# Spreading vector work over the slots of a hand-written order: the first token half behind the last gate and up chunks

## The chip, the cores and the metric

The kernel runs on one core of a Trainium2 chip. Its engines work side by side, each through its own queue of instructions, in order: TensorE (PE in the profile, with the load of its weights shown apart as PEld), VectorE (DVE), ScalarE (ACT), GpSimd (POOL) and SyncE (SP), which here only issues DMA transfers. They wait for each other through semaphores.

The metric is the device time of one execution in microseconds (us), as the median of several runs. A profile is one execution taken by the hardware profiler. Its span runs from the first to the last instruction.

## The reference

Input `x` has 8 batches of 256 tokens with 1024 features, all in float32. Four layers with low-rank adapters (LoRA, rank 16) follow each other, and each adds its result to `x`. Every batch picks its own adapter in each layer.

```python
# layer 0
x = x + (x @ W.T + b + 2.0 * ((x @ A0[id0]) @ B0[id0]))
# layer 1, hidden width F = 2752
gate = x @ W_gate.T + 0.5 * ((x @ A_gate[id1].T) @ B_gate[id1].T)
up   = x @ W_up.T   + 0.5 * ((x @ A_up[id1].T)   @ B_up[id1].T)
act  = silu(gate) * up
x = x + (act @ W_down.T + 0.5 * ((act @ A_down[id1].T) @ B_down[id1].T))
# layers 2 and 3, adapters alone
x = x + (x @ B2[id2].T) @ A2[id2].T
x = x + (x @ B3[id3].T) @ A3[id3].T
```

## The kernel before

**Tiling.** The 2048 tokens are taken in two blocks of 1024 (`blk` 0 and 1), and each block in two halves of 512 tokens (`n` 0 and 1). Layer 0 is done for both blocks, then for each block gate and up, then the down projection with layers 2 and 3. Gate and up are cut along F into chunks of 128; groups of four chunks make a job (`g` 0 to 4). What is left, 64 columns more than 21 chunks, is the remainder: `rest()`, the "last gate and up chunks", named `r` in tile names (`pa_r`, `c_r_X`). It is computed first, ahead of group 0.

**Products.** The large matrix products use a Strassen-like scheme with seven products in place of eight, on two levels. In gate and up the outer seven products are seven units, in the order 1, 2, 3, 5, 6, 7, 4, and each unit's inner seven products are issued by `step` in the order 1, 5, (4 of the unit before), 6, 3, 2, 7. An inner product of a group is four matmuls of 128 x 256; one of the remainder is two. The profile shows each matmul as two records. Inner products write the PSUM banks `pa` (two banks in turn), `pc` and `pb` (one bank each), and each is then added to a result in SBUF (`c_X`, `c_E`, `c_Z`, `c_Y`) by VectorE (lines 509 and 512) or copied there by ScalarE (line 288). Line 478 is the matmul itself. Product 4 of a unit is put into `pending` and issued by `flush()` in slot 2 of the next unit, which also calls `done` when that unit completes a result.

**The remainder's end.** When gate and up of a half are complete (`both` in `done`), these follow: four 32-row expands, one in each group of 32 rows (`lora`, tile `plr`, line 994), into four banks of the pool `ps_l`, which has four; four sums of them onto gate and up (lines 1175, 1176, and 1179 twice); Sigmoids on ScalarE (`gates`); four multiplies (line 1172), of which the last two write `hr`; and `hidden`, a memset, and for the second half also the down-rank products (`shrink_hidden`, tile `pd`, line 263). Before its `lora`, each half needs `trep`: eight ScalarE copies into two banks of `ps_l` and two VectorE multiplies (`spread`, line 1138). The first half completes after remainder unit 5 of 7 (product 6), the second after the last (product 4).

**The order of work.** Each unit has slots, and `at(slot)` first calls what was hooked to the slot, and then takes items from the queue `beside` until their costs reach the unit's share:

```python
            spent = 0
            while beside and spent < u.share:
                cost, f = beside.popleft()
                f()
                spent += cost
```

A cost is a number of the order alone and not a time. An item `(9, lambda: None)` does nothing and uses up the slot. The share is 0.2 or 0.3 in the last remainder units, and 1.1 and 0.8 in the first two units of group 0. So one item of 0.69 fills a slot of the remainder, and two fill a slot of group 0.

The text gives this order; the instructions on an engine may still be placed otherwise by the framework's scheduler, which keeps dependencies. In the kernel before, VectorE's queue has the first half's sums and its first multiply as lines 1175, 1179, 1172, 1176, 1179, while the text calls 1175, 1176, 1179, 1179, 1172.

**Transfers.** Tokens come from DRAM (`toks`) into tiles `tk`, weights into `w_...`, issued by SyncE, one unit or more ahead, into a pool of 22 large buffers that rotate; a load waits until the buffer's last user is done. GpSimd forms the weight sums `sw` (lines 448 to 451) and `w_B`, `w_T` (line 439), one unit ahead, the sums of the down weights `wo` in block 0 (lines 772 to 775), and gathers the adapters' rows (`bgu`, `ad`; line 233), each into two buffers in turn.

Of the kernel before, what the change touches and what calls it, by code (L numbers as in the profile page):

```python
# [54 lines left out]
def kernel(  # L55
# [48 lines left out]
    nc = tc.nc  # L104
# [14 lines left out]
    def big(name):  # L119
        return upool.tile([P, BIG], F32, tag="u", name=name)  # L120

    def bank(pool, name):
        return pool.tile([P, 512], F32, tag=pool.name, name=name)
# [116 lines left out]
    def gather_a(table, layer, blk, name, pool=apool, tag="a", width=NC * R):  # L240
        t = pool.tile([P, BB * width], F32, tag=tag, name=name)
        t = t[:, : BB * table.shape[1]].rearrange("p (b w) -> p b w", b=BB)
        for q in range(BB):
            b = blk * BB + q
            gather(t[:, q, :], table, off_a[:, layer, b : b + 1])
        return t
# [40 lines left out]
    def copy(dst, src, scale=1.0):  # L287
        nc.scalar.activation(dst, src, AF.Identity, scale=scale)  # L288
# [4 lines left out]
    beside = deque()  # L293
# [666 lines left out]
    def gate_up(blk):  # L960
# [5 lines left out]
        def tables(g):  # L966
            b = bgpool.tile([P, 2, NN, P], F32, tag="bg", name=f"bgu_{blk}_{g}")
            for table in range(2):
                for n in range(NN):
                    gather(b[:, table, n], bgu[g], off_gx[:, blk, table, n : n + 1])  # L970
            st["bgu", g] = b
            chunks = ad[g].shape[1] // R
            st["ad", g] = (
                gather_a(ad[g], 1, blk, f"ad_{blk}_{g}", pool=adpool, tag="ad", width=4 * R),
                chunks,
            )

        def shrink_hidden(g, *halves):

            a, chunks = st["ad", g]  # L980
            pss = []
            for n, h in halves:
                pss.append(bank(ps_l, f"pd_{blk}_{g}_{n}"))
                for r in range(len(h)):
                    shrink_into(pss[-1], r, a, chunks, r, n, h[r], True, True)
            for (n, h), ps in zip(halves, pss):
                rows, td = slice(0, 32 * len(h)), st["td"][n]
                if g == REST:
                    nc.vector.memset(td, 0.0)
                nc.vector.tensor_add(td[rows], td[rows], ps[rows])  # L990

        def expand_gu(table, n, g, r, ps):
            rows = slice(32 * r, 32 * r + 32)
            nc.tensor.matmul(  # L994
                ps,
                st["bgu", g][rows, table, n],
                st["t"][rows, table, n, :],
                start=True,
                stop=True,
                skip_group_check=True,  # L1000
            )
# [102 lines left out]
        def rest():  # L1104

            held = {}

            def raw(key, t):
                kh, table = int(key[1]) - 1, int(key[2]) - 1
                if table == 0:  # L1110
                    nc.sync.dma_start(out=t, in_=wrem[kh, 0])
                    return
                nc.sync.dma_start(out=t[:, :512], in_=wrem[kh, 1, :, :512])

                w = t[:, 512:].rearrange("p (c m) -> p c m", m=P)
                for j in range(2):
                    a = st["agu"][j].rearrange("p b (r c) -> p c (b r)", c=NC)
                    nc.scalar.copy(
                        w[:, :, j * BB * R : (j + 1) * BB * R], a[:, kh * HC : (kh + 1) * HC, :]
                    )  # L1120

            def done(n, table, c):
                c = c.rearrange("p q i j t -> p (q i) (j t)")
                held[n, table] = c
                if "t" not in st:
                    st["t"] = big(f"trep_{blk}").rearrange("p (g n t) -> p g n t", g=2, n=NN)
                    st["hr"] = big(f"hr_{blk}").rearrange("p (c n t) -> p c n t", c=2, n=NN)
                t, hr = st["t"], st["hr"]
                lo = []
                ranks, both = c, (n, 1 - table) in held  # L1130

                def spread(j):

                    src = slice(64 * j + 32 * n, 64 * j + 32 * n + 32)
                    ps = bank(ps_l, f"pt_{blk}_{n}_{j}")
                    for r in range(4):
                        copy(ps[32 * r : 32 * r + 32], ranks[src, 1, :], 0.5)
                    nc.vector.tensor_mul(t[:, j, n, :], ps, mask)

                if table == 1:  # L1140
                    for j in range(2):
                        beside.append((0.69, lambda j=j: spread(j)))
                    if both:

                        for _ in range(6):
                            beside.append((9, lambda: None))
                if not both:
                    return
                g, u = held[n, 0], held[n, 1]

                def lora():

                    for j in range(4):
                        lo.append(bank(ps_l, f"plr_{blk}_{n}_{j}"))
                        expand_gu(j // 2, n, REST, j, lo[j])

                def gates():
                    nc.scalar.activation(lo[0], g[:, 0], AF.Sigmoid)
                    nc.scalar.activation(lo[1][:FR], g[:FR, 1], AF.Sigmoid)

                    copy(u[:FR, 1], g[FR:, 1])

                left = slice(0, FR)

                def hidden():
                    nc.vector.memset(hr[FR:, 1, n], 0.0)
                    held["hr", n] = [hr[:, 0, n], hr[:, 1, n]]
                    if ("hr", 1 - n) in held:
                        shrink_hidden(REST, *((n, held["hr", n]) for n in range(NN)))

                def multiply(to, x, y):
                    beside.append((0.69, lambda: nc.vector.tensor_mul(to(), x(), y())))

                beside.append((0, lora))
                beside.append((0.69, lambda: nc.vector.tensor_add(g[:, 0], g[:, 0], lo[0])))
                beside.append((0.69, lambda: nc.vector.tensor_add(u[:, 0], u[:, 0], lo[2])))
                for j, c in ((3, slice(FR, P)), (1, left)):
                    beside.append(
                        (0.69, lambda j=j, c=c: nc.vector.tensor_add(g[c, 1], g[c, 1], lo[j][c]))
                    )  # L1180
                beside.append((0, gates))
                for a, b, c in ((g[:, 0], 0, slice(0, P)), (g[left, 1], 1, left)):
                    multiply(lambda b=b, c=c: lo[b][c], lambda a=a: a, lambda b=b, c=c: lo[b][c])
                multiply(lambda: hr[:, 0, n], lambda: u[:, 0], lambda: lo[0])
                multiply(lambda: hr[left, 1, n], lambda: u[left, 1], lambda: lo[1][left])
                beside.append((1.2, hidden))

            q = Quads(blk, f"1_{blk}_r", 1, raw, done, SHARE_REST)

            def shrink_tables():  # L1190
                st["agu"] = [
                    gather_a(t, 1, blk, f"agu_{blk}_{j}") for j, t in enumerate((ag, au))
                ]

            q.units[0].ahead.insert(0, (3, 0, shrink_tables))
            q.units[0].before(2, 0, lambda: tables(REST))
# [500 lines left out]
```

## Time and profile before

| | |
|---|---|
| median of 3 runs | 1817.87 us (1817.19 to 1818.16) |
| profiled execution, its own time | 1794.66 us |
| its span | 1792.7 us |
| granted TensorE clock | 0.998 |
| TensorE busy | 1779.4 us (99%) |
| VectorE busy | 1039.3 us (58%) |
| GpSimd busy | 1007.1 us (56%) |
| ScalarE busy | 306.6 us (17%) |
| remainder's end, block 0 and block 1 | about 265 to 288 us and 1044 to 1066 us from the span's start |

A row of the list in order of time shows the start, the duration, the engine, the line, the operation with output and inputs, the count, and in brackets the idle time before it with what ended that. Matmuls are pipelined and their ends are modelled, so a busy TensorE is not one at its peak, and the distance from start to start tells more than a duration. An engine is idle at no cost where TensorE doesn't wait for it.

### The profile page before, as it was taken

The page shows a single profiled execution, that of the slowest core. Times are in us where ns is not written, and L with a number is a line of the kernel's source. Part 1 is how long each engine was busy: PE and PEld are TensorE (multiplying, and loading weights), DVE is VectorE, ACT ScalarE, POOL GpSimd, SP SyncE. Part 2 cuts the span into 40 slices and gives each one's busy share as a digit, 9 for nine tenths or more (in the row PEclk, how much of TensorE's full clock was granted, in tenths as well). Part 3 has the DMA queues.
Part 4 walks back from the last instruction along what each step waited for, and adds up shares of the span by engine and source line. Part 5 has one row for each costly group of instructions (what it writes and reads, how often), then busy time and mean ns, then how long its engine had stood idle before and what let it go on. Part 6 is the DMA issues. An engine that isn't in the chain of part 4 may idle for free.

```text
span 1792.7 us, 20768 instructions
## 1 busy us (share of the span) xinstructions
PE 1779.4 (99%) x7664; PEld 1310.9 (73%) x7664; DVE 1039.3 (58%) x1675; ACT 306.6 (17%) x552; POOL 1007.1 (56%) x807
## 2 busy tenths in 40 slices
PE   9999999999999999999999999999999999999998
PEld 4444477888787888788854678787888887888743
DVE  5584256666666666757842474757575757544623
ACT  0121023020212121224210231111212121221001
POOL 6202579685868677344631777766767564444302
PEclk9999999999999999999999999999999999999999
DMA  6476895867686756678831885575748475645302
GB/s 235 174 282 247 275 393 186 314 223 291 208 298 207 297 182 235 250 270 323 321 128 60 293 325 194 175 281 175 293 169 292 162 259 179 252 168 187 125 0 94
DMA packets 119446, 404.42 MB, mean 226 GB/s; under 512 B 11890, under 2 KB 42738, under 8 KB 109874
## 3 DMA queue, kind: packets, MB, share of 16 engines
q1 hardware_dynamic: 108464, 381.72, 58.7%
q0 software_dynamic: 6288, 13.77, 2.4%
q10 hardware_dynamic: 4594, 7.61, 1.3%
q8 instruction: 62, 1.02, 0.2%
q14 instruction: 38, 0.31, 0.0%
HBM read 318.64 MB, written 84.41 MB: 225 GB/s over the span
## 4 chain that ended last, share of the span: by engine, by line
PE 91%; issue 5%; DVE 3%; POOL 0%; ACT 0%; POOLq 0%; ACTq 0%; DVEq 0%
PE pa L478 27%; PE pc L478 13%; PE pa_d L478 11%; PE pa L377 8%; PE pb L478 6%; PE pc_d L478 5%; PE pc L377 4%; PE pb_d L478 3%; PE pa_r L478 2%; PE pl L994 2%; PE pb L377 2%; PE pp L880 2%; PE pc_r L478 1%; PE pd L263 1%; PE p L263 1%
## 5 line engine op out<-in xcount | busy, mean ns | idle before, releaser
L478 PE MATMUL pa<-tk,sw 128*128 128x256 f32 x1120 | 270.3, 384 | 0.0
L478 PE MATMUL pc<-tk,sw 128*128 128x256 f32 x1120 | 264.6, 379 | 0.0
L478 PEld LDWEIGHTS pa<-tk,sw 128*128 128x128 f32 x1120 | 209.8, 190 | 58.2 <-issue 9.9
L478 PEld LDWEIGHTS pc<-tk,sw 128*128 128x128 f32 x1120 | 212.8, 190 | 28.9
L478 PE MATMUL pa<-tk,w_B 128*128 128x256 f32 x960 | 227.8, 380 | 0.0
L478 PEld LDWEIGHTS pa<-tk,w_B 128*128 128x128 f32 x960 | 181.6, 190 | 32.5 <-issue 8.2
L448 POOL TENSOR_TENSOR sw<-w_B 128x512 f32<-128x512 f32 x60 | 76.4, 1273 | 167.8 <-PE pa L478 148.6
L619 POOL TENSOR_TENSOR dx_d<-dw_d 128x512 f32<-128x512 f32 x28 | 37.3, 1354 | 159.1 <-PE pa L478 41.5
L478 PE MATMUL pb<-tk,w_B 128*128 128x256 f32 x480 | 113.4, 379 | 0.0
L478 PE MATMUL pa_d<-dh_d,dw_d 128*128 128x256 f32 x448 | 102.6, 380 | 0.0
L478 PE MATMUL pc_d<-dh_d,dw_d 128*128 128x256 f32 x448 | 101.6, 379 | 0.0
L478 PEld LDWEIGHTS pb<-tk,w_B 128*128 128x128 f32 x480 | 91.2, 190 | 12.4
L509 DVE TENSOR_TENSOR c_X<-c_X,pa 128x512 f32<-128x512 f32 x90 | 61.3, 681 | 65.2 <-PE pa L478 65.2
L439 POOL TENSOR_TENSOR w_B<-w_B,w_B 128x1024 f32<-128x1024 f32 x40 | 93.5, 2361 | 2.4 <-PE pa L478 2.4
L478 PEld LDWEIGHTS pa_d<-dh_d,dw_d 128*128 128x128 f32 x448 | 85.5, 191 | 12.6 <-issue 0.8
L478 PEld LDWEIGHTS pc_d<-dh_d,dw_d 128*128 128x128 f32 x448 | 85.1, 190 | 11.6
L450 POOL TENSOR_TENSOR sw<-w_B 128x512 f32<-128x512 f32 x60 | 87.7, 1461 | 0.0
L451 POOL TENSOR_TENSOR sw<-w_B,sw 128x512 f32<-128x512 f32 x60 | 80.7, 1345 | 3.9
L449 POOL TENSOR_TENSOR sw<-sw,w_B 128x512 f32<-128x512 f32 x60 | 77.0, 1284 | 0.0
L288 ACT ACTIVATE c_X<-pa 128x512 f32<-128x512 f32 x30 | 17.7, 589 | 340.2 <-PE pa L478 340.2
L233 POOL DMA_INDIRECT ad<-in_ad_dram,off_a x48 | 46.1, 960 | 29.2 <-PE pd L263 18.4
L377 PE MATMUL pa<-ht,wd 128*128 128x512 f32 x128 | 59.6, 598 | 0.0
(386 smaller groups left out, 3133.0 us busy)
## 6 DMA issues: line engine op xcount, KB each, us to landing
tk<-toks SPq DMA_DIRECT2D x140, 896.0 KB, 6.7
w_B<-in_wgu_dram SPq DMA_DIRECT2D x40, 1024.0 KB, 5.1
tk_r<-toks SPq DMA_DIRECT2D x28, 896.0 KB, 9.5
hk<-c_Z SPq DMA_DIRECT2D x32, 512.0 KB, 4.2
dh_d<-hk SPq DMA_DIRECT2D x14, 1024.0 KB, 8.7
hk<-c_Y SPq DMA_DIRECT2D x24, 512.0 KB, 4.6
x1d<-x SPq DMA_DIRECT2D x8, 1024.0 KB, 6.7
wo<-in_wd_dram SPq DMA_DIRECT2D x8, 1024.0 KB, 7.0
```

The source lines that it names most:

```text
L233: nc.gpsimd.indirect_dma_start(out=t, out_offset=None, in_=table, in_offset=bass.IndirectOffsetOnAxis(ap=off, axis=0),)
L263: nc.tensor.matmul(ps[32 * r : 32 * r + 32, :], v, src, start=start, stop=stop, skip_group_check=True)
L377: nc.tensor.matmul(ps, v[j], m[j], start=start and k == 0, stop=k == len(moving) - 1, skip_group_check=True,)
L439: f(self.raw[out][:, c], self.raw[a][:, c], self.raw[b][:, c])
L448: nc.gpsimd.tensor_add(s1, m21, m22)
L449: nc.gpsimd.tensor_sub(s2, s1, m11)
L450: nc.gpsimd.tensor_sub(s3, m11, m21)
L451: nc.gpsimd.tensor_sub(s4, m12, s2)
L478: nc.tensor.matmul(ps[:, q, :], w(j, q, kk), tok(j, kk), start=start and q == 0 and kk == 0, stop=kk == self.deep - 1, skip_group_check=True,)
L509: nc.vector.tensor_add(view(out, r, k), view(old, r, k), ps)
L619: nc.gpsimd.tensor_sub(s3[:, c], a11[:, c], a21[:, c])
L880: nc.tensor.matmul(pss[j, n], st["w", o][:, i, j // HC], x[c][n], start=i == 0, stop=i == NC - 1,)
```

## The change

In `rest()`, each vector operation behind a half's expands is appended through a new helper, `vector`. For the first half (`n == 0`) the helper appends an empty item of cost 9 behind each operation. That makes eight empty items per token block: behind the four sums and the four multiplies. Operands and operations stay as they are, and the second half's items are appended as before.

```diff
+                def vector(f):
+                    beside.append((0.69, f))
+                    if n == 0:
+
+                        beside.append((9, lambda: None))
+
                 def multiply(to, x, y):
-                    beside.append((0.69, lambda: nc.vector.tensor_mul(to(), x(), y())))
+                    vector(lambda: nc.vector.tensor_mul(to(), x(), y()))
 
                 beside.append((0, lora))
-                beside.append((0.69, lambda: nc.vector.tensor_add(g[:, 0], g[:, 0], lo[0])))
-                beside.append((0.69, lambda: nc.vector.tensor_add(u[:, 0], u[:, 0], lo[2])))
+                vector(lambda: nc.vector.tensor_add(g[:, 0], g[:, 0], lo[0]))
+                vector(lambda: nc.vector.tensor_add(u[:, 0], u[:, 0], lo[2]))
                 for j, c in ((3, slice(FR, P)), (1, left)):
-                    beside.append(
-                        (0.69, lambda j=j, c=c: nc.vector.tensor_add(g[c, 1], g[c, 1], lo[j][c]))
-                    )
+                    vector(lambda j=j, c=c: nc.vector.tensor_add(g[c, 1], g[c, 1], lo[j][c]))
                 beside.append((0, gates))
```

## The prediction

> **What bounds the kernel now.** I read the page first, for the bound, then the list of the matmul engine's work in order of time around the place that is edited, then the same stretch for all engines.
>
> ```profile
> span 1792.7 us, 20768 instructions
> ...
> PE 1779.4 (99%) x7664; PEld 1310.9 (73%) x7664; DVE 1039.3 (58%) x1675; ACT 306.6 (17%) x552; POOL 1007.1 (56%) x807
> ...
> PE 91%; issue 5%; DVE 3%; POOL 0%; ACT 0%; POOLq 0%; ACTq 0%; DVEq 0%
> ```
>
> TensorE is busy for 99% of the span and holds 91% of the chain that ended last, at a granted clock of 0.998. So an edit is worth what it adds to or takes from TensorE's own sequence; VectorE (DVE) counts only where TensorE waits for it. Next, TensorE alone, at the end of the last gate and up chunks of token block 0 (start, duration, instruction):
>
> ```profile
> 276.08 1.03 PE L478 MATMUL pa_r<-tk_r,w_r_B 128*128 128x256 f32 x4
> 277.03 2.16 PE L994 MATMUL plr<-trep,bgu 32*128 32x512 f32 x8
> 279.12 1.99 PE L478 MATMUL pa<-tk,sw 128*128 128x256 f32 x8
> 280.95 1.89 PE L478 MATMUL pc<-tk,sw 128*128 128x256 f32 x8
> ...
> 284.40 1.89 PE L478 MATMUL pa<-tk,sw 128*128 128x256 f32 x8
> 286.22 1.91 PE L263 MATMUL pd<-hr,ad 128*32 128x512 f32 x8
> 288.07 1.99 PE L478 MATMUL pa<-tk,w_B 128*128 128x256 f32 x8
> 289.90 1.89 PE L478 MATMUL pc<-tk,sw 128*128 128x256 f32 x8
> ```
>
> Ends are modelled, so I use starts alone. A block of four products (8 records) takes 1.73 us from start to start, for example 282.68 to 284.40; the half-size block `pa_r` takes half, 0.86. The four second-half expands `plr` cost what is left between 276.08 and 280.95: 4.87 - 0.86 - 1.73 = **2.28 us**. Token block 1 has the same stretch at 1054.45 to 1059.32: also 4.87, so 2.28. The down-rank products `pd` cost 289.90 - 284.40 - 2 x 1.73 = 2.04 us. Here is an expand of the same four-matmul form where nothing is late, two units later:
>
> ```profile
> 303.71 1.89 PE L478 MATMUL pa<-tk,w_B 128*128 128x256 f32 x8
> 305.53 1.14 PE L994 MATMUL pl<-trep,bgu 32*128 32x512 f32 x8
> 306.60 1.99 PE L478 MATMUL pa<-tk,sw 128*128 128x256 f32 x8
> 308.43 0.81 PE L478 MATMUL pc<-tk,sw 128*128 128x256 f32 x3
> ```
>
> It costs 308.43 - 303.71 - 2 x 1.73 = **1.26 us**. The difference of 1.02 us is explained by the list for all engines (in brackets the idle time before and its releaser):
>
> ```profile
> 271.65 0.73 PEld L478 LDWEIGHTS pa_r<-tk_r,sw_r 128*128 128x128 f32 x4 [2.00 <-DVE c_r_X L509]
> ...
> 276.14 0.69 DVE L1138 TENSOR_TENSOR trep<-pt,mask 128x512 f32<-128x512 f32 x1 [1.17 <-ACT pt L288]
> ...
> 276.75 1.27 DVE L1172 TENSOR_TENSOR hr<-c_r_Z,plr 128x512 f32<-128x512 f32 x2
> 277.03 0.74 PEld L994 LDWEIGHTS plr<-trep,bgu 32*128 32x128 f32 x6 [0.33 <-DVE trep L1138]
> ...
> 278.07 0.29 PEld L994 LDWEIGHTS plr<-trep,bgu 32*128 32x128 f32 x2 [0.30 <-DVE hr L1172]
> ...
> 279.03 0.68 DVE L1175 TENSOR_TENSOR c_r_X<-c_r_X,plr 128x512 f32<-128x512 f32 x1
> ```
>
> The second-half expands wait for `trep`, which ends at 276.83, just before them, and the last of them for the fourth PSUM bank, which the first half's last multiply into `hr` gives back at about 278.0. The first line of the fence is the stall that the edit seems to be about: the first half's sums stand ahead of an accumulate (L509) that TensorE needs, and it loses 271.66 - 269.04 - 0.86 = 1.76 us (1050.03 - 1048.08 - 0.86 = 1.09 us in block 1).
>
> **The change part by part.** Nothing is computed more or less: eight vector operations per token block, for n == 0, each get an empty item of cost 9 behind them. [...]
>
> *First part, the first half's sums.* In the order of the text they go to slots 3, 5 and 7 of the last remainder unit (3 to 7 before) and to the next chunk's first unit. In the order in which the two built programs issue on VectorE, nothing moves up to and including the last `trep`: the two L1175/L1179 sums, the L1172 multiply, L1176, L1179, then the L509 that TensorE waits for. The scheduler behind the text puts them there in both. So the 1.76 and 1.09 us stay. Value: **0**.
>
> *Second part, what queues behind them.* `lora` for the second half is appended when the last remainder product is done, so it now stands behind the paused items. On TensorE the four `plr` matmuls move from before product 6 of the next chunk's first unit to behind its product 7, four blocks later (the 6.92 us from 276.94 on), and `pd` from before the second unit to behind that unit's product 6. At the new place all that `plr` needs is old: `trep` from 276.83, the last multiply into `hr` by about 279. It then costs like `pl`, 1.26 instead of 2.28: **-1.02 us** per token block. `pd` still stands between full-size blocks, 2.04 us as before: 0. The sum is 2 x -1.02 = -2.04 us.
>
> Here one rule is weighed. The row says 1.26 us for an expand with its banks free. The Trainium skill, TensorEngine Tiling (Array Packing), under Key Properties, says that different tiles run in parallel and that a change of tiling mode drains the engine. By parallel tiles alone, four 32-row matmuls would take as long as one full 512-column matmul, and those here run four in 3.43 us, 0.86 each (103.09 to 106.52 in the chain); the sum would be 2 x (0.86 - 2.28) = -2.84 us. I take the row, since it holds the drain on both sides too, and keep -2.84 as the low end. The drain is also what would speak against moving a block; but `plr` and `pd` are each entered and left as often as before.
>
> *Third part, VectorE at the new place.* This is the new wait. The second unit's product 6 needs the bank that its product 1 filled and `c_E<-c_X,pa` (L509) reads, and in the new VectorE order that add is behind seven of the eight second-half operations. With times carried over from before: `pa_r` at 276.08, four blocks, `plr` at 283.95, the second unit's product 1 at 283.95 + 1.07 = 285.02, then 1.83 (a first block behind another mode, 306.60 to 308.43) and 2 x 1.73, so product 6 wants to start at 290.31. VectorE's first sum starts 1.16 us behind `plr` (306.69 against 305.53), at 285.11. Such operations follow each other at 0.60 us when independent and 0.70 when not (279.03, 279.63, 280.23, 280.93, 281.65). Sum 285.11, sum 285.71, Sigmoid on ScalarE 285.82 to 286.42, multiply 286.45, sum 287.06, sum 287.76, multiply 288.36, multiply into `hr` 288.96, the L509 add 289.6 to 290.29. That is 0.02 us ahead of its need, and 0.06 us pass from such an end to a matmul's start. So I count +0.05 us per block. Bounds: 0 if VectorE keeps 0.60 throughout, +0.45 if all seven take 0.70. None of the eight reads SBUF alone, the kind that stretched to 1.28 us next to GpSimd at 259.08, so I stay near the low bound. Behind the add come the last multiply into `hr` (291.0, needed by `pd` at about 292.1) and the add of bank `pc` (291.7, needed by product 3 at 294.0): covered by 1 and 2 us.
>
> *Fourth part, the queues.* ScalarE: the copy of the first unit's product 6 now stands ahead of the second-half Sigmoids, needed at 282.13 and ready from 279.5; no second table load is added. GpSimd: the `ad` gathers (4 x 1.25 us) wait for `pd` and move behind the third unit's weight sums (and `wo`'s, in block 0), so those sums start about 5 us sooner; the fourth unit's sums stay where they were, near 310, and are needed at 315.5: cost 0, and without that cover each us would count. `bgu` waits for `plr`, and GpSimd, free at 284.9, for 0.2 us of it. SyncE: same order. In block 0 one token load waits for product 7 (283.9) instead of a multiply (282.9), and the queue's next entry comes at 305.7; in block 1 one waits for the second half's last multiply, some 5 us later than before, for a unit that starts about 40 us after that. Cost 0.
>
> **Sum.** -2.04 + 2 x 0.05 = -1.9 us against the profiled execution's 1794.66 us (span 1792.7). The runs' median lies 23.2 us above that execution; nothing in the edit touches what lies between, so the same difference holds: 1817.87 - 1.9 = **1816.0 us**, 0.10% less. Faster or slower by 0.2% (3.6 us) is about what this kernel's measurement can tell from no change.
>
> **Rivals.**
> *The gain is used up* (chance 0.24). The saved 1.02 us returns as a wait, through the +0.45 bound of the third part together with an expand that keeps half of its wait for a bank (0.5). For it: the margin of 0.02 us. Against: pairs of VectorE operations at 0.60. Time: 1817.87 - 2.04 + 2 x 0.95 = 1817.7, no change.
> *VectorE becomes the bound in the second unit* (0.08), the case on the other side. Place: the L509 add behind seven second-half operations. Price: 2 us in total per us of lateness. It ends slower than before from 1.02 us of lateness on, and slower by 0.2% from 2.8 us on. At 3 us: 1817.87 - 2.04 + 6 = 1821.8. For it, VectorE's in-order queue; against, it would need the seven operations to take about 1.0 us each where rows show 0.67 to 0.70. I give 0.05 to beyond 0.2%.
> *The sums really spread out* (0.06), what the edit says it does, and the first half's stall goes too: 1817.87 - 1.9 - 1.76 - 1.09 = 1813.1, 0.26% faster. Against it stands the unchanged VectorE order up to `trep`. That the text changes the slots and that queue not at all is the forecast's own premise.
>
> **How the numbers follow.** The forecast has 0.62, its own range 1815.0 (the -2.84 bound) to 1816.9. To hold 8 in 10 I reach up over most of the used-up gain, to 1818.3, and down to 1814.6 for half a microsecond of scatter below the low bound (the three runs lie within 1.0). Faster by over 0.2%: 0.05, nearly all of the third rival. Slower by over 0.2%: 0.05, from the second. The rest, 0.90, is within.
>
> **What would show it.** In the profile after: `plr` of the second half behind four blocks `pa`, `pc`, `pb`, `pa` of the next chunk, with about 1.1 us to the next block's start instead of 2.1; the 2.00 us line before `pa_r` unchanged; `pd` behind the second unit's product 6 at its old cost; no new idle time before `pa<-tk,sw` in the second unit. The forecast is wrong if TensorE shows a wait on L509 `c_E` there of half a microsecond or more, if the `pa_r` stall shrinks, or if the span changes elsewhere, since only these instructions and the `ad` gathers change place.

## The result and the profile after

The changed kernel takes 1815.72 us (median of 22 runs, 1814.35 to 1818.11), the kernel before 1817.3 us beside it (22 runs). The ratio is 0.9992, 95% interval 0.9987 to 0.9998: about 1.6 us faster, between 0.4 and 2.4. A second measurement of the same two kernels (21 and 25 runs, the last below) gave 0.9993, 0.9986 to 0.9999.

The first lines of the page of the changed kernel:

```profile
span 1814.4 us, 20766 instructions
...
PE 91%; issue 5%; DVE 3%; POOL 0%; ACT 0%; POOLq 0%; ACTq 0%; DVEq 0%
```

TensorE still sets the time. The span must not be compared with the 1792.7 us before: the profiled execution of the changed kernel holds some 23 us that the other lacks, all in its first 61 us. The view of stretches shows it (busy time of each engine, then granted clock, DMA share and GB/s):

```profile
33.00:61.00 28.00, 15.47 (x34) 2.67 (x32) 0.00 (x0) 0.00 (x0) 15.94 (x17) 0.63 0.11 31
```

TensorE is busy for 15.5 of these 28 us at a mean clock of 0.63; in the profile before the same stretch was 28.00 busy at 1.00. This is not the edit, which issues its first different instruction more than 200 us later; the last run below takes it up. So I compare stages, by TensorE's starts.

The end of the last gate and up chunks of token block 0 after the change, TensorE alone (start, duration, instruction, and in brackets the idle time before it with its releaser):

```profile
294.64 1.13 PE L478 MATMUL pa_r<-tk_r,sw_r 128*128 128x256 f32 x4 [1.59 <-DVE c_r_X L509]
...
305.11 1.89 PE L478 MATMUL pa<-tk,sw 128*128 128x256 f32 x8
306.93 1.14 PE L994 MATMUL plr<-trep,bgu 32*128 32x512 f32 x8
308.00 1.99 PE L478 MATMUL pa<-tk,w_B 128*128 128x256 f32 x8
309.83 1.89 PE L478 MATMUL pc<-tk,sw 128*128 128x256 f32 x8
311.55 1.89 PE L478 MATMUL pa<-tk,w_B 128*128 128x256 f32 x8
313.63 1.97 PE L478 MATMUL pa<-tk,sw 128*128 128x256 f32 x8 [0.18 <-issue]
315.52 1.91 PE L263 MATMUL pd<-hr,ad 128*32 128x512 f32 x8
317.37 1.99 PE L478 MATMUL pc<-tk,sw 128*128 128x256 f32 x8
```

Three things are to be read. The stall ahead of `pa_r` is unchanged: 1.59 us in the bracket in both kernels. The second half's expands now cost 309.83 - 305.11 - 2 x 1.73 = 1.26 us. And one block is late: `pa<-tk,sw` at 313.63, the second unit's product 6, starts 2.08 us behind the one before it, where such blocks of this kernel take 1.73. With "issue" the view names no releaser; the list of VectorE shows which add it is:

```profile
308.08 0.69 DVE L1181 TENSOR_TENSOR c_r_X<-c_r_X,plr 128x512 f32<-128x512 f32 x1 [0.36 <-PE plr L994]
308.69 0.67 DVE L1184 TENSOR_TENSOR c_r_X<-c_r_X,plr 64x512 f32<-64x512 f32 x1
309.44 0.69 DVE L1178 TENSOR_TENSOR plr<-c_r_X,plr 128x512 f32<-128x512 f32 x1
310.04 0.68 DVE L1182 TENSOR_TENSOR c_r_Y<-c_r_Y,plr 128x512 f32<-128x512 f32 x1
310.76 0.69 DVE L1184 TENSOR_TENSOR c_r_X<-c_r_X,plr 64x512 f32<-64x512 f32 x1
311.48 0.69 DVE L1178 TENSOR_TENSOR plr<-c_r_X,plr 64x512 f32<-64x512 f32 x1
312.20 0.69 DVE L1178 TENSOR_TENSOR hr<-c_r_Y,plr 128x512 f32<-128x512 f32 x1
312.80 0.68 DVE L509 TENSOR_TENSOR c_E<-c_X,pa 128x512 f32<-128x512 f32 x1
```

The add that gives product 6 its bank is the last line. It runs behind seven of the second half's eight operations and ends at 313.48, 0.15 us ahead of the late start; a run below, in which another block is late in the same way, names such an add in its bracket. (The lines of the eight operations are six higher than in the kernel before: L1172 is L1178 here.)

All runs are compared by one stage time: from the start of the remainder product `pa_r<-tk_r,w_r_T` ahead of the first half's expands to the start of the next expands `pl`, for each token block.

| | block 0 | block 1 | against before | timed ratio, 95% interval |
|---|---|---|---|---|
| before | 40.58 | 40.76 | | |
| changed | 39.99 | 40.16 | -0.59, -0.60 | 0.9992, 0.9987 to 0.9998 |
| second half held back alone | 39.99 | 40.16 | -0.59, -0.60 | 0.9991, 0.9983 to 1.0000 |
| expands one product later | 40.00 | 40.17 | -0.58, -0.59 | 0.9992, 0.9983 to 1.0000 |
| expands two products later | 39.57 | 39.75 | -1.01, -1.01 | 0.9992, 0.9984 to 1.0001 |
| both halves paused | 39.99 | 40.16 | -0.59, -0.60 | 0.9993, 0.9984 to 1.0001 |
| first half later | 43.12 | 42.81 | +2.54, +2.05 | 1.0016, 1.0009 to 1.0022 |
| both halves later | 42.80 | 43.08 | +2.22, +2.32 | 1.0013, 1.0006 to 1.0019 |
| the same, four copies on VectorE | 42.15 | 40.54 | +1.57, -0.22 | 0.9996, 0.9988 to 1.0004 |
| the same, eight copies on VectorE | 39.15 | 38.73 | -1.43, -2.03 | 0.9976, 0.9966 to 0.9985 |
| changed, once more | 39.99 | 40.34 | -0.59, -0.42 | 0.9993, 0.9986 to 0.9999 |

So the edit is worth -1.19 us in the trace: per block -1.02 for the expands, +0.35 for the late product 6, +0.07 lost behind it (from product 6 to `pd` 1.89 us, and 1.82 before). The timed difference of -1.6, between -0.4 and -2.4, agrees. The timed ratios of the first five kernels behind "before" can't tell 1.2 from 2.0 us. Their stage times can: the gains of both blocks agree to 0.01 us, and so do those of kernels in which the same block is late. The one that strays is block 1 of the changed kernel's second profile, by 0.18 us.

### The profile page after: what moved, and what is told of

Same layout as the page of the kernel before. It is cut to its first block, busy times and chain, and to the rows that moved or that the text cites. A ratio compares the mean times of both kernels' runs of the same rounds, so it can differ in the third digit from the quotient of the medians.

```text
span 1814.4 us, 20766 instructions
## 1 busy us (share of the span) xinstructions
PE 1788.1 (99%) x7664; PEld 1310.4 (72%) x7664; DVE 1040.8 (57%) x1675; ACT 306.8 (17%) x552; POOL 1005.6 (55%) x807
## 3 DMA queue, kind: packets, MB, share of 16 engines
q8 instruction: 62, 1.02, 0.2%
## 4 chain that ended last, share of the span: by engine, by line
PE 91%; issue 5%; DVE 3%; POOL 0%; ACT 0%; POOLq 0%; ACTq 0%; DVEq 0%
PE pa L478 26%; PE pc L478 13%; PE pa_d L478 11%; PE pa L377 8%; PE pb L478 6%; PE pc_d L478 5%; PE pc L377 4%; PE pb_d L478 3%; PE pa_r L478 2%; PE pl L994 2%; PE pb L377 2%; PE pp L880 2%; PE pc_r L478 1%; PE pd L263 1%; PE t L263 1%
## 5 line engine op out<-in xcount | busy, mean ns | idle before, releaser
L509 DVE TENSOR_TENSOR c_X<-c_X,pa 128x512 f32<-128x512 f32 x90 | 61.3, 681 | 65.2 <-PE pa L478 65.2
```

Source lines behind the costliest of these rows:

```text
L509: nc.vector.tensor_add(view(out, r, k), view(old, r, k), ps)
```

## The experiments

Each edit is against the kernel before, except where another is named.

**Second half held back alone.** The first half's sums keep their slots.

```diff
                 beside.append((1.2, hidden))
+                if n == 0:
+                    for _ in range(5):
+                        beside.append((9, lambda: None))
```

> The first half's sums keep their slots; only the second half's work is held back, by five empty items behind the first half's last one. Theory (all that the change is worth comes from the later place of the second half's expands, less the lateness of the add behind them): the same as the changed kernel, -1.3 us against the kernel before (-0.57 us in block 0 and -0.74 us in block 1, from the start of pa_r to the second unit's second product); second half's expands 1.26 us; the wait ahead of pa_r stays at 1.59 and 0.93 us in the rows; the second unit's product 6 starts 2.08 us behind the product before it. Rival (spreading the first half's own operations is worth something): the gain is smaller than 0.5 us, or the wait ahead of pa_r is another.

Measured: -0.59 and -0.60 us, the same as the changed kernel to 0.01 us; the wait ahead of `pa_r` 1.60 and 0.93; the expands 310.86 - 306.14 - 3.46 = 1.26; product 6 at 314.67, 2.08 us behind the block before. The expectation held, but for the -0.74 us that it had for block 1. What the change says in its loop, that every other slot stays free between the first half's operations, is worth nothing; that the second half stands behind it is worth everything.

**Expands one and two products later.** Six and seven empty items in place of five.

```diff
-                    for _ in range(5):
+                    for _ in range(6):     # and 7 in the other run
```

> As the first, with six empty items: the second half's expands come one product later, behind the second unit's first product, and the add that product 6 needs is ahead of the eight operations; now the add behind product 5 (bank pc) has seven of them ahead of it, and the product that needs that bank comes three blocks behind the expands. Theory (lateness is that of an add with seven operations ahead of it, three blocks behind the expands): product 6 is on time, the product in bank pc that follows it is late by 0.35 us instead, total -1.3 us. Rival (lateness belongs to product 6, or to the change of shape there, not to VectorE's queue): no late product, each block gains the full 1.02, total -2.0 us; or product 6 is still 0.35 us late.

> Seven empty items: the expands come behind the second unit's product 5, and both adds whose banks the next blocks need are ahead of the eight operations. The first add behind the eight is needed four blocks and the down-rank products later. Theory: no late product anywhere; expands at 1.26 us; -1.02 us per block in full, total -2.0 us. Rival (the 0.4 us per block lies elsewhere, in shorter steps lost round the new place): total stays at -1.3 us.

TensorE in block 0, one product later:

```profile
308.83 1.14 PE L994 MATMUL plr<-trep,bgu 32*128 32x512 f32 x8
309.90 1.99 PE L478 MATMUL pc<-tk,sw 128*128 128x256 f32 x8
311.73 1.89 PE L478 MATMUL pa<-tk,w_B 128*128 128x256 f32 x8
313.46 1.89 PE L478 MATMUL pa<-tk,sw 128*128 128x256 f32 x8
315.54 1.97 PE L478 MATMUL pc<-tk,sw 128*128 128x256 f32 x8 [0.19 <-DVE c_E L509]
```

and two products later:

```profile
311.24 1.14 PE L994 MATMUL plr<-trep,bgu 32*128 32x512 f32 x8
312.31 1.99 PE L478 MATMUL pa<-tk,w_B 128*128 128x256 f32 x8
314.14 1.89 PE L478 MATMUL pa<-tk,sw 128*128 128x256 f32 x8
315.87 1.89 PE L478 MATMUL pc<-tk,sw 128*128 128x256 f32 x8
317.59 1.89 PE L478 MATMUL pb<-tk,w_B 128*128 128x256 f32 x8
```

With one product more, product 6 (313.46) is on time and the block in bank `pc` behind it is late, 2.08 us again, three blocks behind the expands; here the bracket names `c_E` L509. With two products more nothing is late: every step is 1.73, or 1.83 behind another shape, and the block gives -1.01, the whole of what the expands save. So the lateness belongs to VectorE's queue: an add with seven of the eight operations ahead of it whose bank is needed three blocks behind the expands. With two products more, the first add behind the eight is not needed until behind `pd`.

**Both halves paused.** The pauses of the changed kernel for n == 1 too, so that `pd` comes behind the second unit's last product.

```diff
# against the changed kernel
                 def vector(f):
                     beside.append((0.69, f))
-                    if n == 0:
-
-                        beside.append((9, lambda: None))
+                    beside.append((9, lambda: None))
```

> The changed kernel with the pauses behind the second half's operations too. The order of the adds and of the eight operations on VectorE is that of the changed kernel up to the third add of the second unit; only the down-rank products pd come later, behind the second unit's last product. Theory: pd costs 2.04 us wherever it stands between full blocks, product 6 is 0.35 us late as in the changed kernel, total -1.3 us. Rival (pd close behind product 6 is what costs the 0.42 us per block, as it waits for the last multiply into hr): product 6 or the block behind it is on time, total -2.0 us.

Measured -0.59 and -0.60; product 6 at 312.83, 2.08 us behind the block before it, as in the changed kernel; the next block, now `pc` and not `pd`, 1.80 us behind it. The place of `pd` is worth nothing, and the 0.07 us behind product 6 belong to its late start.

**First half later, and both.** The prediction had priced the stall ahead of `pa_r` at 1.76 and 1.09 us, as what a real spreading out would bring. Here it is taken away by issuing the first half's expands behind the last remainder adds.

```diff
-                        for _ in range(6):
+                        for _ in range(10):
                             beside.append((9, lambda: None))
...
                 beside.append((1.2, hidden))
+                if n == 0:                         # the second run only
+                    for _ in range(5):
+                        beside.append((9, lambda: None))
```

> Ten empty items instead of six ahead of the first half's expands, and no pauses: the first half's expands come behind the last remainder unit's product in bank pa, so that on VectorE every remainder add that TensorE waits for stands ahead of the first half's sums. Theory (the stall ahead of pa_r is the queue order on VectorE, which the change left as it was): the rows of 1.59 and 0.93 us go, -1.76 us in block 0 and -1.09 us in block 1, total -2.9 us; the second half's expands keep their wait for trep and a bank (about 2.3 us). Rival (the lost time comes back, since the second half's work is then queued behind a later first half): expands of the second half at 3 us or more, or a wait in the next chunk's first unit, total between 0 and -1 us.

> Ten empty items ahead of the first half's expands, and five behind its last item: the first half's expands as in the run before, the second half's behind the second unit's product 5, where no add that TensorE needs soon stands behind the eight operations. Theory: the two gains add, -2.9 us from the stall and -2.0 us from the second half's expands, total -4.9 us, 0.27% less. Rival (one gain contains the other, or the later places collide): total near -3 us or less.

Both came out slower than the kernel before, by 3.0 and 1.8 us of the medians: both expectations fell. TensorE in block 0 of the first of them, and then its ScalarE:

```profile
293.85 1.03 PE L478 MATMUL pa_r<-tk_r,sw_r 128*128 128x256 f32 x4
...
299.44 1.03 PE L478 MATMUL pa_r<-tk_r,w_r_B 128*128 128x256 f32 x4
300.30 0.59 PE L478 MATMUL pb<-tk,w_B 128*128 128x256 f32 x2
303.70 3.52 PE L478 MATMUL pa<-tk,sw 128*128 128x256 f32 x8 [2.80 <-ACT c_X L288]
307.05 1.89 PE L478 MATMUL pc<-tk,sw 128*128 128x256 f32 x8
```

```profile
296.69 0.60 ACT L1158 ACTIVATE plr<-c_r_E 128x512 f32<-128x512 f32 x1 [5.37 <-DVE c_r_E L1175]
297.28 0.59 ACT L1159 ACTIVATE plr<-c_r_E 64x512 f32<-64x512 f32 x1
298.70 1.22 ACT L288 ACTIVATE pt<-c_r_Y 32x512 f32<-32x512 f32 x2 [0.83 <-DVE c_r_Z L1176]
299.94 0.63 ACT L288 ACTIVATE c_r_Z<-c_r_E 64x512 f32<-64x512 f32 x1
300.60 2.44 ACT L288 ACTIVATE pt<-c_r_Y 32x512 f32<-32x512 f32 x4
302.98 0.57 ACT L288 ACTIVATE c_X<-pa 128x512 f32<-128x512 f32 x1
```

The stall is gone: the `pa_r` at 293.85 has no bracket. In its place TensorE stands from 300.73 (two matmuls of `pb` behind 300.30) to 303.70, 2.97 us, for the copy `c_X<-pa`, which gives back the bank of the first unit's product 1. In ScalarE's list that copy is behind the first half's Sigmoids, which now start later, and six copies `pt` of the second half. The same copy in the changed kernel:

```profile
299.03 0.57 ACT L288 ACTIVATE c_X<-pa 128x512 f32<-128x512 f32 x1
```

It ended there at about 299.6, 0.3 us ahead of the block that needs it (299.93): the stall ahead of `pa_r` had been hiding a ScalarE queue that was late by almost as much.

Then `pa` itself takes 307.05 - 303.70 = 3.35 us in place of 1.73. The stretches:

```profile
300.70:303.70 3.00, 0.20 (x2) 0.03 (x1) 1.25 (x3) 2.93 (x6) 3.00 (x3) 0.95 0.69 215
303.70:307.00 3.30, 3.30 (x8) 2.68 (x9) 2.62 (x5) 1.51 (x3) 3.30 (x2) 0.52 1.03 399
```

After 3 us of standing still, TensorE's granted clock is 0.52 over the next 3.3 us, and 1.6 us more are lost. The block's sum is -1.76 (stall) - 1.02 (the second half's expands, whose `trep` is old here too) + 2.97 + 1.62 + 0.56 (a wait for an add ahead of another `pa_r`, which the first half's expands had covered) + 0.31 (`pd`) = +2.7; steps of about 0.1 us round the first half's expands give back the rest to the measured +2.54. In the second run the second half's expands had nothing left to gain.

The half clock came in both blocks of both profiles. The timed differences, 3.0 and 1.8 us, are smaller than the stages' +4.6 and +4.5 us, and the granted clocks point to why: 0.9913 and 0.9916 in the mean over the runs of these two kernels, and 0.9925 for the kernel before beside them. As an estimate from these means, the two lose 2.2 and 1.7 us per run more to a low clock than the kernel before, which is about 1.3 and 1.0 such periods where the profiles hold two.

**Copies taken off ScalarE.** If ScalarE's queue holds the bank, fewer `pt` copies ahead must bring the copy forward by their number. Against the run "both halves later":

```diff
-                        copy(ps[32 * r : 32 * r + 32], ranks[src, 1, :], 0.5)
+                        if table == 1 and n == 1 and j == 1:   # four; without j == 1: eight
+                            nc.vector.tensor_scalar_mul(
+                                ps[32 * r : 32 * r + 32], ranks[src, 1, :], 0.5
+                            )
+                        else:
+                            copy(ps[32 * r : 32 * r + 32], ranks[src, 1, :], 0.5)
```

> The run before (first half's expands behind the remainder's last product in bank pa, second half's behind the second unit's product 5), with four of the eight 0.61 us copies pt of the second half made by VectorE in place of ScalarE. In the run before, the copy of the first unit's first product out of bank pa stood on ScalarE behind two Sigmoids, six pt copies and one more copy, TensorE's product 6 started 3.40 us behind the end of pa_r, and TensorE then ran 3.4 us at half clock (1.6 us lost). Theory (ScalarE's queue holds the bank, and the half clock follows from TensorE's standing still): two pt copies fewer are ahead, product 6 is 2.2 us late in place of 3.4, the half clock does not come, and block 0 goes from +2.2 us to about -0.6 us against the kernel before. Rival (the weight sums on GpSimd, which follow a weight load, set product 6): it stays 3.4 us late, with the half clock, total near +4 us again.

> As the run before, with all eight pt copies of the second half on VectorE. Theory (ScalarE's queue): the copy out of bank pa follows the Sigmoids and one copy, 3.7 us sooner than with eight on ScalarE; product 6 is about 1.0 us late, no half clock; block 0 at -1.8 us (-1.76 for the stall ahead of pa_r, -1.02 for the second half's expands, +1.0), total -3 us in two blocks, if VectorE's eight copies of some 0.6 us delay no add that TensorE waits for. Rival (GpSimd's weight sums): product 6 still 3.4 us late. Second rival (the delay only changes its engine: VectorE is late now): a wait on an add or on trep of 1 us or more.

TensorE with four copies moved, block 0 and then block 1:

```profile
273.52 1.03 PE L478 MATMUL pa_r<-tk_r,w_r_B 128*128 128x256 f32 x4
276.56 2.51 PE L478 MATMUL pa<-tk,sw 128*128 128x256 f32 x8 [2.01 <-ACT c_X L288]
278.87 3.07 PE L478 MATMUL pc<-tk,sw 128*128 128x256 f32 x8
281.77 1.89 PE L478 MATMUL pb<-tk,w_B 128*128 128x256 f32 x8
...
1053.37 1.03 PE L478 MATMUL pa_r<-tk_r,w_r_B 128*128 128x256 f32 x4
1056.40 1.97 PE L478 MATMUL pa<-tk,sw 128*128 128x256 f32 x8 [2.01 <-ACT c_X L288]
1058.20 1.89 PE L478 MATMUL pc<-tk,sw 128*128 128x256 f32 x8
```

and with eight:

```profile
274.79 1.03 PE L478 MATMUL pa_r<-tk_r,w_r_B 128*128 128x256 f32 x4
276.03 1.97 PE L478 MATMUL pa<-tk,sw 128*128 128x256 f32 x8 [0.21 <-ACT c_X L288]
...
286.56 1.62 PE L994 MATMUL plr<-trep,bgu 32*128 32x512 f32 x8
288.12 1.99 PE L478 MATMUL pa<-tk,w_B 128*128 128x256 f32 x8
```

From the end of `pa_r` (its start and 0.86) to product 6 there are 3.40 us with no copy moved, 2.18 with four (2.2 was expected) and 0.38 with eight (1.0 was expected). In block 1, where only five copies `pt` stood ahead and not six, it is 2.79, 2.17 and 0.38 us. Each copy taken away from ahead is worth 0.61 us, until the wait is nearly gone. The cause is shown: it is ScalarE's queue, not the weight sums on GpSimd. One part of the expectation fell: with four copies moved the half clock still came in block 0 (`pc` takes 2.90 us from start to start), though not in block 1 after an equal pause of 2.17 us. With its 1.7 us, and the 0.56 us wait ahead of the other `pa_r` that the expectation had left out, block 0 came to +1.57 and not to -0.6. Timed, the kernel is at 0.9996, at most 1.0004, which has no room for the stages' +1.35 us; -0.40 without the half clock would fit. The mean clock of its runs, 0.9979 against 0.9981 before, points to few half-clock periods as well. With eight copies moved it came behind this wait in neither block. There VectorE makes the copies at 0.71 us each, and the second rival shows a little: in block 0 the second half's expands take 288.12 - 286.56 = 1.56 us in place of 1.07, as `trep` is late.

The kernel with eight copies moved took 1789.28 us against 1793.47 for the kernel before beside it: 0.9976, interval 0.9966 to 0.9985. By the stages it gains 3.5 us where the change gains 1.2. The changed kernel was not timed beside it, but its interval, 0.9987 to 0.9998, lies wholly above this one.

**The pause at the start.**

> The changed kernel once more, for its start: in its first profile TensorE stood or ran at half clock for some 23 us in the first 61 us, in L263, which the kernel before did not show in its profile. Theory (the pause belongs to the chip of that run, not to the change): where the kernel before takes about 1793 us on the same chip, the changed kernel takes about 1792 us and its profile shows no pause; where the kernel before takes about 1817 us, both have it. The two token blocks again give -0.6 us each. Rival (the change brings the pause): the changed kernel is some 23 us slower than the kernel before on a chip where that one takes 1793 us.

Here the kernel before took 1816.46 us and the changed one 1814.55. Its profile has the pause too: in the stretch from 33 to 61 us TensorE was busy for 15.56 us at a clock of 0.70. The case that would have shown it best, the changed kernel where the kernel before takes 1793 us, did not come up. But the kernel before itself took 1793.47 us in the group of the two runs above and 1816.46 to 1817.87 us in the others, so the step of 23 us is there without the edit. In the profile of the kernel with eight copies moved, which is of that group, TensorE is busy for all 28.00 us of that stretch, at a clock of 1.00. No profile of the kernel before holds the pause; for it only the times show the step. The group at 1793 us ran on another chip than the groups ahead of it and behind it, but also at another time, so what brings the pause stays open. Block 1 gave -0.42 in this run and not -0.60: its first-half expands waited 0.59 us for `trep`, 0.18 more than in the other profile.

## Why the prediction was right, point by point

*First part, value 0.* Right. The brackets ahead of `pa_r` are 1.59 and 0.93 us in both kernels, and holding back the second half alone gives the whole result. The reading that decided it was the order in which the built kernel issues on VectorE, not the slots of the text.

*Second part, -1.02 us per block.* Right to 0.01: the expands cost 1.26 us at the new place, the same as the row `pl` that stood for them. Parallel tiles alone, which would have made it 0.86, are not the whole cost: 0.40 us more were measured. Whether that is the drain was not tested. Taken alone, as with the expands two products later, this part gives -1.01 and -1.01.

*Third part, +0.05 us per block.* This is the term that was mis-sized: it measured 0.35 us at product 6 and 0.07 behind it, near the upper bound of 0.45. The place was right, the add L509 behind seven operations, and so was the start (1.15 us behind `plr`). The working counted the steps behind the second 64-row sum at 0.60 us. Two of them took 0.72: that to the multiply of 64 rows (310.76 to 311.48) and that to the first multiply into `hr` (311.48 to 312.20). Neither reads what stands just ahead: the multiply's rows were summed at 308.69, and ScalarE's Sigmoid of them started at 309.45, ahead of the sum at 310.76.

The kernel before had these steps in its rows. The second 64-row sum works on rows 64 to 127, every other operation of the chain starts at row 0, and there too the steps to that sum and behind it took 0.70 and 0.72 us (280.23 to 280.93 to 281.65), though a multiply of 128 rows follows. The step to the first multiply into `hr` goes with it (0.71 us in the kernel before, where the two multiplies ahead start at 281.65 and 282.25 and it at 282.96). It is the first operation behind that sum to write SBUF, since the multiply between writes PSUM. In the first half an L509 add writes SBUF between, and the step behind the 64-row multiply is 0.59 us:

```profile
294.17 0.42 DVE L509 TENSOR_TENSOR c_r_X<-c_r_X,pa_r 128x256 f32<-128x256 f32 x1
294.51 0.68 DVE L1178 TENSOR_TENSOR plr<-c_r_E,plr 64x512 f32<-64x512 f32 x1
295.10 0.40 DVE L512 TENSOR_TENSOR c_r_X<-c_r_X,pc_r 128x256 f32<-128x256 f32 x1
```

So in this chain the long step goes with a change of the row at which operations start, and not with a result just ahead. That is read from the rows; no run was made to test it.

The add ended 0.21 us later than the working had it, and 0.15 us, not 0.06, passed to TensorE's start. With a margin of 0.02 us all of it showed.

*Fourth part, queues at 0.* Right: the only new bracket on TensorE's matmuls in the stage is that of product 6. It is also a sign that the prediction had not foreseen ("no new idle time" there), though short of the half microsecond that it named as being wrong.

*The sum.* -1.9 was predicted, the stages give -1.19 and the times -1.6, with an interval that holds both. That 1816.0 us was predicted and 1815.72 measured is closer than the working deserves, by luck: beside the changed kernel the kernel before took 1817.3 us and not 1817.87, and these 0.57 us stand against the gain that was missing. The step from the profiled execution to the median, 23.2 us taken as the same for both, was right as well. It has the size of the pause at the start, which the profile of the kernel before happened to lack.

*Rivals.* The gain used up: in part, 0.42 of 1.02 us came back, and through the first of the two causes that it named; the expands kept no wait for a bank. VectorE as the bound of the second unit: no. The sums really spread out: no; and its price was wrong besides. It took the stall ahead of `pa_r` as a gain of 1.76 and 1.09 us, but where the stall was taken away by later sums, ScalarE's copy was the next thing late, and that cost more.

## What to carry to other kernels

Where a stall of the bounding engine is to be removed, look up what its other suppliers finish just in time behind it: here a copy on ScalarE was ready 0.3 us ahead of its need, so taking away a stall of 1.76 us by moving work back made the kernel slower until that queue was shortened too. Work that is moved later can land ahead of someone else's buffer release in an engine's queue; here, moving it two products further cost nothing and made that wait vanish. Where a chain of vector operations has a margin of hundredths of a microsecond, take each step from a row of the same operation behind the same one: the two steps that were missed here, 0.72 us and not 0.60, could be read in the kernel before.

## What the runs showed of the hardware that was not expected

In the profiles TensorE's clock fell to about half behind pauses of 2.8 to 3.0 us (four of four) and of 2.2 us (one of two), for one period of about 3.4 us each time, which cost 1.6 to 1.7 us on top of the pause. Behind the stall of 1.76 us in the seven profiles that keep it, the blocks went on at 1.73 us. The Trainium skill, TensorE: Matmul & The Clock Gate, Part 1, has the gate close after an idle window of about 3.4 us which runs free of the kernel; these pauses were shorter, so no such window fits whole into one of them, and the measurement decides. That the window runs free could be why equal pauses differ; this was not tested.

Single periods of 3.4 us at half clock also came with TensorE busy: one at 754 to 760 us in the changed kernel (mean clock 0.72 there), one at 1510 to 1516 us in the kernel before (0.72). Each costs about 1.7 us, more than the whole effect, which is why differences of spans were not used. What brings them is open.
